# First experts and first head by halves of tokens, and weights requested at other moments, in a hybrid attention and expert stack

## The chip, the cores and the metric

The kernel runs on one core of one Trainium2 chip. Its time is the device time of one execution in microseconds; three executions were timed and the median is the measure. A profile of one more execution was taken with the hardware profiler. The engines are called PE (TensorE), DVE (VectorE), ACT (ScalarE), POOL (GpSimd) and SP (SyncE, which here only issues DMAs).

## What is computed

There are 1024 tokens of 512 numbers. Four layers follow each other, each on the layer norm of its input, added to that input:

```python
x = x + attention_a(layernorm(x), wq, bq, wk, bk, wv, bv, wo, bo)   # 32 heads of 16, 8 groups of keys
x = x + ffn(layernorm(x), W_base, b_base, W_router, A, B)
x = x + attention_b(layernorm(x), scales_q, ..., qw_q, qw_k, qw_v, qw_o)
x = x + ffn(layernorm(x), W_base, b_base, W_router, A, B)           # same weights again
```

Attention B has 32 heads of 128 in 8 groups of keys and values, is causal, and holds its weights as whole numbers 0 to 15, to be shifted by 8 and scaled per 128 input rows:

```python
w = (qw.astype(float32) - 8) * repeat(scales, 128, axis=0)
q, k, v = x @ w_q, x @ w_k, x @ w_v            # then rotary embedding of q and k:
q = q * cos + concat(-q[64:], q[:64]) * sin    # (per head; k likewise)
attn = softmax(where(causal, q @ k.T / sqrt(128), min))
out = (attn @ v) @ w_o
```

The feed-forward layer is one dense product and a low-rank part of rank 16 with 8 experts of which each token takes the best two:

```python
base = xf @ W_base.T + b_base
rw, sel = top_k(xf @ W_router.T, 2);  rw = softmax(rw)
lora = einsum('ter,te,eor->to', einsum('td,erd->ter', xf, A), onehot_weights(rw, sel), B) * 2
```

## The kernel before

The kernel has four stages on one core: attention A up to about 480 us, the first experts from 484 to about 535, attention B with its 32 heads to about 1418, and the second experts to the end.

**Who sets the order.** In attention B and both experts the order of PE's instructions is the order of the source. DVE, ACT, POOL and SP are ordered by the scheduler of the tile framework, which puts an instruction where its inputs and buffers are due; each engine then works through its own queue in order. A DMA that SP issues must wait, with everything behind it in SP's queue, until its source is written and its target buffer is free.

**First experts** (class `Experts`, L577 to L670). For each of eight tiles of 128 tokens, `hidden` computes the low-rank rows and the router's logits (L595), `route` picks the two experts on DVE for a range of tiles, `turned` transposes the weighted rows (evacuated by L134), `base` is the dense product (L607) and `finish` adds the low-rank product (L668) and adds the sum to x (L670). Each quarter of x (two tiles) that is complete is written to `x_kept` in DRAM, normalized (`ready`, L149 to L162), and turned into `x_hl`, a high and a low part of x transposed (`halves_of_x`, L185 and L754 to L756). Before, routing was done for tiles 0 to 5 and then for 6 and 7.

**Attention B's projections.** `whole_numbers` loads raw weights r from DRAM (L705, on SP) and POOL makes w = r - 8 from them (L706). Buffers: two of r and two of w for queries and for keys with values, one of r and two of w for the output weights. `scaled` multiplies w with x_hl, high and low part in turn (L798, L799), one PSUM bank for each 128 input rows, and gathers the four with their scales (L810 on ACT for the first, L812 on DVE for the others). `rotated` does it for 512 tokens at a time, then exchanges the halves of the head by two DMAs (`turned`, L822 and L823), and computes acc * cos + turned * sin in three operations (L824 to L826): on POOL, except for the queries of head 0, which are rotated on DVE.

**A head.** `probabilities(n, t)` computes the scores of query tile t of 128 tokens (L869), the mask and the row maximum in one DVE operation (L877), and the exponential on ACT (L881). `divided` is a reciprocal of the row sums (L885) and a scaling on ACT (L886). `placed` transposes 32 x 32 blocks on DVE (L900), and behind an odd tile of a pair four DMAs move the blocks to their rows (L911). `context` multiplies them with the values (L949), and `project_out` with the output weights (L798, L799), gathered on DVE into yT (L983). The scores have one wide PSUM buffer and one narrow one; five PSUM banks serve all else.

**The written order.** For each head, eight turns: `TURNS` gives the order of tiles, 0, 6, 1, 7, 2, 4, 3, 5, and head 0 had its own, 0, 1, 2, 4, 3, 5, 6, 7. Between scores, `fill` takes shares of other work from two lists, `short` (projections) and `long` (context and turned values); `advance` takes one step of one of their items and `complete` the whole. The tiles of `x_sb` are reused for the probabilities, in the slots named by `SLOTS` and `LAST`.

**Requests of weights.** At the start of head n, the source requested the query and output weights of head n+1, and at certain heads the keys' or values' weights of the next group (L1076 to L1083). The experts' weights lay in `shared` until attention B took that space; they are kept in DRAM (`w_kept`) and come back into the space of `x_hl` by one load after the last head's turns (L1137, L1138).

## Time and profile before

| what | us |
|---|---|
| three runs | 1474.58, 1474.74, 1477.38 |
| median | 1474.74 |
| profiled execution | 1478.29 |
| span of its instructions | 1476.5 |
| PE busy | 1398.8 (95%) |
| DVE busy | 1228.7 (83%) |
| ACT busy | 832.4 (56%) |
| POOL busy | 460.6 (31%) |

The span is the time from the first to the last instruction of the profiled execution, and the execution's own time has 1.8 us around it. A line such as `pc L949` means an instruction of line 949 of the kernel which writes the tile `pc`. In a timeline, the first two numbers are the start and the duration, and brackets hold the time that the engine sat idle before it and what ended that wait. `SPq` stands for SP's queue. Busy times are averages over stages; the stages are read from windows. The granted clock (PEclk) is the share of full speed that PE was given in a window.

### The profile page before, as it was taken

To read this page: it belongs to the slowest core of one execution; us is meant where nothing else is said; L and a number is where in the kernel's file an instruction comes from. 1 tells how busy PE (TensorE), PEld (TensorE's weight loads), DVE (VectorE), ACT (ScalarE), POOL (GpSimd) and SP (SyncE) were. 2 spreads that over 40 slices of the span, in tenths; PEclk is the share of its full clock that TensorE was granted. 3 is DMA by queue.
4 is the path that set the end of the run, shared out by engine and by line. 5 is a ranking of instruction groups with operands and counts; after the bars stand their busy time and mean duration, and the time that the engine had idled before them with its cause. 6 is when DMAs were issued, how large, how long until landed. Compare 5 with 4: busy or idle time off the path is not lost.

```text
span 1476.5 us, 21101 instructions
## 1 busy us (share of the span) xinstructions
PE 1398.8 (95%) x6711; PEld 884.2 (60%) x6711; DVE 1228.7 (83%) x2546; ACT 832.4 (56%) x1580; POOL 460.6 (31%) x363
## 2 busy tenths in 40 slices
PE   6999999999999998999999999999999999999788
PEld 4444444444444555677776776776776766777564
DVE  4799979889891668799998998998998989989683
ACT  2176757666676335765655655655665655666420
POOL 3200000000000516536445355445445535433120
PEclk9999999999999999999999999999999999999999
DMA  4352414223330415555555555545655555555511
GB/s 124 59 104 46 68 34 70 45 50 60 53 118 2 126 57 143 138 135 147 146 136 134 138 133 140 146 119 143 154 126 130 137 144 128 131 134 155 137 45 57
DMA packets 135870, 158.46 MB, mean 107 GB/s; under 512 B 34912, under 2 KB 111392, under 8 KB 135504
## 3 DMA queue, kind: packets, MB, share of 16 engines
q1 hardware_dynamic: 135340, 156.49, 44.6%
q8 instruction: 54, 0.88, 0.2%
q0 software_dynamic: 352, 0.59, 0.1%
q14 instruction: 56, 0.46, 0.1%
q10 hardware_dynamic: 68, 0.03, 0.0%
HBM read 33.03 MB, written 6.05 MB: 26 GB/s over the span
## 4 chain that ended last, share of the span: by engine, by line
PE 63%; DVE 15%; DMA 9%; ACT 4%; issue 3%; POOL 3%; SPq 3%; DVEq 0%; ACTq 0%; POOLq 0%
PE pc L949 11%; PE sc L869 10%; PE po L408 7%; PE sc L334 7%; DVE m L343 6%; DMA xT<-blocks 5%; PE pp L798 4%; PE pp L799 3%; PE bank L607 3%; DMA turned<-acc 3%; PE py L798 2%; PE py L799 2%; SPq L911 2%; PE st L375 2%; PE py L448 2%
## 5 line engine op out<-in xcount | busy, mean ns | idle before, releaser
L343 DVE TENSOR_REDUCE m<-sc 128x1 f32<-128x512 f32 x512 | 319.8, 682 | 25.8 <-PE st L375 20.1
L387 ACT ACTIVATE pT<-st 128x512 f32<-128x512 f32 x512 | 264.7, 602 | 128.6 <-PE st L383 115.6
L869 PE MATMUL sc<-kT,qT 128*128 128x512 f32 (+3 forms) x768 | 291.4, 488 | 4.1 <-DVE qT L826 1.7
L949 PE MATMUL pc<-xT,v_sb 128*128 128x256 f32 (+1 forms) x1024 | 243.4, 364 | 28.5 <-DMA xT<-blocks 26.0
L881 ACT ACTIVATE x_sb<-x_sb,m 128x768 f32<-128x768 f32 (+7 forms) x256 | 196.9, 769 | 124.8 <-DVE m L877 121.0
L886 ACT ACTIVATE x_sb<-x_sb,total 128x768 f32<-128x768 f32 (+7 forms) x256 | 194.2, 770 | 120.1 <-DVE total L885 120.0
L949 PEld LDWEIGHTS pc<-xT,v_sb 128*128 128x128 f32 x1024 | 192.0, 191 | 65.7 <-issue 28.7
L877 DVE CUSTOM_DVE_ANT_0 x_sb<-sc,causal 128x768 f32<-128x768 f32 (+7 forms) x256 | 191.2, 747 | 34.1 <-PE sc L869 33.5
L334 PE MATMUL sc<-ks,qs 64*128 64x512 f32 x512 | 186.8, 448 | 5.3 <-DVE m L343 2.5
L798 PE MATMUL pp<-x_hl,w 128*128 128x512 f32 x384 | 185.6, 483 | 5.9 <-ACT acc L810 5.2
L869 PEld LDWEIGHTS sc<-kT,qT 128*128 128x128 f32 x768 | 138.9, 192 | 75.6 <-issue 61.2
L383 PE MATMUL st<-ms_q,ones 64*128 64x512 f32 x512 | 178.0, 413 | 0.7 <-DMA ms_q<-mT 0.7
L375 PE MATMUL st<-qs,ks 64*128 64x512 f32 x512 | 175.9, 423 | 1.4
L983 DVE SCALAR_TENSOR_TENSOR shared<-py,o_sc,shared 128x512 f32<-128x512 f32 x248 | 173.8, 731 | 2.0 <-PE py L799 2.0
L334 PEld LDWEIGHTS sc<-ks,qs 64*128 64x128 f32 x512 | 83.8, 184 | 146.1 <-DVE m L343 129.5
L824 POOL TENSOR_TENSOR qT<-acc,cos_sb 128x512 f32<-128x512 f32 x62 | 79.8, 1287 | 248.6 <-DVE acc L812 246.4
L799 PE MATMUL pp<-x_hl,w 128*128 128x512 f32 x384 | 154.0, 401 | 2.4 <-DVE x_hl L756 2.4
L900 DVE STREAM_TRANSPOSE blocks<-x_sb 128x640 f32<-128x640 f32 (+3 forms) x128 | 133.3, 1041 | 21.4 <-ACT x_sb L886 14.7
L706 POOL TENSOR_SCALAR w<-r 128x512 fp32r<-128x512 int32 x80 | 119.4, 1492 | 93.8 <-PE pp L799 49.7
L812 DVE SCALAR_TENSOR_TENSOR acc<-pp,q_sc,acc 128x512 f32<-128x512 f32 x192 | 140.3, 731 | 9.6 <-ACT acc L810 8.7
L798 PE MATMUL py<-ctx,w 128*128 128x512 f32 x256 | 133.6, 522 | 3.4 <-DVE shared L983 1.1
L408 PE MATMUL po<-pT,v_sb 128*32 128x512 f32 x1024 | 136.6, 604 | 0.0
(171 smaller groups left out, 1889.2 us busy)
## 6 DMA issues: line engine op xcount, KB each, us to landing
xT<-blocks SPq DMA_DIRECT2D x128, 240.0 KB, 4.4
xT<-blocks SPq DMA_DIRECT2D x128, 176.0 KB, 3.4
turned<-acc SPq DMA_DIRECT2D x160, 128.0 KB, 2.7
pT<-x_sb SPq DMA_DIRECT2D x128, 112.0 KB, 2.5
qs<-q_hl SPq DMA_DIRECT2D x128, 64.0 KB, 2.4
qs<-shared SPq DMA_DIRECT2D x128, 64.0 KB, 2.5
r<-in_qwq_dram SPq DMA_DIRECT2D x32, 256.0 KB, 2.8
r<-in_qwo_dram SPq DMA_DIRECT2D x32, 256.0 KB, 2.8
```

The lines of the kernel that those rows point to most:

```text
L334: nc.tensor.matmul(sc, qs[pair % NS][rows, jj, ts(t, P)], ks[pair // 2 % NS][rows, ts(half, C)], start=True, stop=True,)
L343: nc.vector.tensor_reduce(ms[pair][:, at : at + 1], sc, AX.X, ALU.max, negate=True)
L375: nc.tensor.matmul(st, ks[pair // 2 % NS][rows, ts(kt, P)], qs[pair % NS][rows, u // 2, ts(u % 2, C)], start=True, stop=False,)
L387: nc.scalar.activation(pTs[pair, kt][:, u], st, AF.Exp, scale=DA**-0.5)
L408: nc.tensor.matmul(po[ts(u, 32), :], v_sb[:, kt, pair // 2, :], pT[:, u], start=(kt == 0), stop=(kt == NT - 1),)
L798: nc.tensor.matmul(ps, lhsT, high, start=True, stop=False)
L799: nc.tensor.matmul(ps, lhsT, low, start=False, stop=True)
L869: nc.tensor.matmul(sc[:, k0:k1], qT[:, ts(t, P)], kT[:, k0:k1], start=True, stop=True)
L877: nc.vector.tensor_tensor_reduce(p, sc[:, :keys], causal[:, S - keys :], -1.0, BIG, ALU.add, ALU.min, m)
L881: nc.scalar.activation(p, p, AF.Exp, bias=m, scale=-1.0, accum_out=total)
L886: nc.scalar.activation(p, p, AF.Copy, scale=total)
L949: nc.tensor.matmul(pc[:, 2 * P * i + lo : 2 * P * (i + 1)], v_sb[:, k, ts(g, DB)], some, start=(k == 0), stop=(k == 2 * pair + 1),)
```

## The change

1. Weights: the queries' raw weights of heads 0 and 1 are requested at the start; those of head n+1 at the start of head n as before, from head 1 on; the output weights of head n at its third turn; the keys' and values' weights at the fifth turn of the head before the one in which they were requested (`request`).
2. First experts: routing is done by halves, tiles 0 to 3 and 4 to 7; the two tiles of a quarter are computed and finished together; the normalized rows lie in a part of `v_sb` in place of tiles of their own.
3. First head: the first halves (512 tokens) of the keys, of queries 0 and of queries 1 are issued within the experts (`half_of`), and the first four query tiles of head 0, which need only the first half, stand ahead of the last quarter of x and of the second halves. The second half of the keys of group 0 is rotated on DVE and not on POOL. Head 0 takes its tiles in order 0 to 7, with the wide scores buffer for the odd ones; `SLOTS` is 0, 1, 3.
4. The experts' weights come back in seven pieces of at most 128 x 517 numbers, one in each of the last head's turns but the first (`reload`); each is behind a one-column copy on DVE which ties it to that turn's row sums.

```diff
@@ weights at the start
-            wqs = {0: input_weights("q", qwq, 0)}
+            wqs = {n: input_weights("q", qwq, n) for n in range(2)}
@@ keys
-                yield from rotated(kTs[g], wks.pop(g), lambda c: k_sc[:, c, g : g + 1])
+                engines = nc.gpsimd, nc.gpsimd if g else nc.vector
+                yield from rotated(kTs[g], wks.pop(g), lambda c: k_sc[:, c, g : g + 1], engines)
@@ probabilities
-                wide = t >= NT // 2 or (n == 0 and t == 1)
+                wide = t >= NT // 2 or (n == 0 and t % 2 == 1)
-            SLOTS = 0, 3, 1
+            SLOTS = 0, 1, 3
@@ first experts
-                    xns = [sb.tile([P, 2, C], F32, name=f"xn{i}") for i in range(2)]
+                    xns = [v_sb[:, 2 * i : 2 * i + 2, C:] for i in range(2)]
+                    def half_of(lane, name):
+                        item = [q for q in lane if q[0] == name][0]
+                        for _ in range(5):
+                            advance(lane, item)
-                    moe.route(0, 6)
-                    moe.route(6, 8)
...
+                    moe.route(0, 4)
...
+                    moe.finish(3)
+                    ready(1)
+                    moe.route(4, 8)
...
-                    for item in list(short):
-                        while advance(short, item):
-                            pass
+                    half_of(short, ("k", 0))
+                    half_of(short, ("q", 0))
                     moe.finish(6)
                     moe.finish(7)
                     ready(3)
                     halves_of_x(2, xns[0])
-                    short.append([("v", 0), 16 * FAST, values(0)])
-                    for _ in range(4):
-                        advance(short, short[-1])
-                    halves_of_x(3, xns[1])
+                    half_of(short, ("q", 1))
@@ before the heads
+                def reload(i, total):
+                    flat = x_hl.rearrange("p i c s -> p (i c s)")
+                    room = place_ffn_weights(flat.bitcast(F32))
+                    width = -(-room.shape[1] // (NT - 1))
+                    part = slice(i * width, min((i + 1) * width, room.shape[1]))
+                    nc.vector.tensor_copy(flat[:, part.start : part.start + 1], total)
+                    nc.sync.dma_start(room[:, part], w_kept[:, part])
+                def request(n):
+                    g, j = n // J, n % J
+                    if j == 0 and 0 < g < G - 1:
+                        wks[g + 1] = input_weights("k", qwk, g + 1)
+                    if j == 2 and g + 1 < G:
+                        wvs[g + 1] = input_weights("k", qwv, g + 1)
+                divided(*turn(0, 0))
+                divided(*turn(0, 1))
+                half_of(short, ("v", 0))
+                halves_of_x(3, xns[1])
+                divided(*turn(0, 2))
+                complete(("k", 0))
+                complete(("q", 0))
+                divided(*turn(0, 3))
+                complete(("v", 0))
+                complete(("q", 1))
+                wks[1] = input_weights("k", qwk, 1)
@@ a head
-                        wqs[n + 1] = input_weights("q", qwq, n + 1)
-                        wos[n + 1] = whole_numbers("o", qwo[ts(n + 1, P), :], C)
+                    if 0 < n < HEADS - 1:
+                        wqs[n + 1] = input_weights("q", qwq, n + 1)
+                        if n and i == 2:
+                            wos[n] = whole_numbers("o", qwo[ts(n, P), :], C)
+                        if i == 4:
+                            request(n + 1)
                         fill(short, shares[0])
                         divided(p, total)
+                        if n == HEADS - 1 and i:
+                            reload(i - 1, total)
@@ after the heads
-                weights = place_ffn_weights(x_hl.rearrange("p i c s -> p (i c s)").bitcast(F32))
-                nc.sync.dma_start(weights, w_kept)
```

`turn(n, t)` issues the scores and exponential of one tile, and places the tile before it, as the loop did.

## The prediction

> **What bounds the kernel now.** I read the page first: the busy shares, then the chain of work that ended last.
>
> ```profile
> span 1476.5 us, 21101 instructions
> ...
> PE 1398.8 (95%) x6711; PEld 884.2 (60%) x6711; DVE 1228.7 (83%) x2546; ACT 832.4 (56%) x1580; POOL 460.6 (31%) x363
> ...
> PE 63%; DVE 15%; DMA 9%; ACT 4%; issue 3%; POOL 3%; SPq 3%; DVEq 0%; ACTq 0%; POOLq 0%
> ```
>
> TensorE is busy 95% of the span, so at most 1476.5 - 1398.8 = 77.7 us is idle time, and an edit that does not change the matmuls can only win from it. The average hides where it lies, so I asked next for windows around the two places that the diff touches. Columns: from:to, length, busy us of PE, PEld, DVE, ACT, POOL, then granted TensorE clock, DMA share, GB/s.
>
> ```profile
> 540.00:560.00 20.00, 15.77 (x55) 10.45 (x53) 17.23 (x37) 10.24 (x20) 9.16 (x7) 0.83 0.29 92
> 560.00:580.00 20.00, 15.78 (x60) 9.88 (x59) 18.79 (x38) 14.05 (x23) 13.78 (x11) 1.00 0.51 128
> ...
> 1360.00:1380.00 20.00, 13.24 (x47) 10.11 (x46) 11.78 (x27) 6.48 (x12) 4.06 (x4) 0.83 0.71 210
> ```
>
> There are two weak places. From 540 to 580 (last of the first experts, first head of attention B) PE loses 8.4 of 40 us while VectorE is at 17.2 and 18.8 of 20: VectorE is the bound there. From 1360 to 1380 (head 30 to head 31) PE loses 6.8 us and VectorE idles too, while the DMA engines are at 0.71: a transfer bounds it. The timeline of PE names the waits, in square brackets behind an instruction:
>
> ```profile
> 543.19 0.80 PE L799 MATMUL pp<-x_hl,w 128*128 128x512 f32 x1 [2.38 <-DVE x_hl L756]
> 562.10 1.35 PE L869 MATMUL sc<-kT,qT 128*128 128x512 f32 x4 [1.73 <-DVE qT L826]
> 1370.93 1.62 PE L949 MATMUL pc<-xT,v_sb 128*128 128x256 f32 x3 [6.76 <-DMA xT<-blocks]
> ```
>
> A long wait costs twice. In the windows after the first and the third of these the granted clock is 0.50 for 3.41 us or twice that:
>
> ```profile
> 543.04:546.45 3.41, 2.56 (x6) 1.59 (x6) 3.41 (x10) 0.86 (x2) 0.00 (x0) 0.50 0.12 49
> 1369.08:1372.50 3.42, 1.57 (x4) 1.33 (x5) 0.00 (x0) 0.00 (x0) 0.88 (x1) 0.50 0.74 192
> ```
>
> Last, the waits in the steady heads (620 to 1385), on PE and in SyncE's queue (total, times, longest):
>
> ```profile
> PE pc L949 <- DMA xT<-blocks: 20.7, 12, 6.8
> ```
> ```profile
> SPq L705 <- POOL w L706: 140.0, 67, 11.3
> ```
>
> So in 30 heads PE waits 20.7 us for turned blocks of probabilities, and SyncE stands 140 us behind raw-weight loads that wait for a buffer which GpSimd has not yet converted.
>
> **The change part by part.** The sum is made on the profiled execution, 1478.29 us (span 1476.5 and 1.8 around it), which lies 3.55 above the median of 1474.74; differences are carried over to the median.
>
> *Raw weights at other moments (L1076, L1077, L1080, L1083).* Comparing the built programs engine by engine, from the end of the first head to the start of the last one PE's instructions stand in the same order, GpSimd's too but for one swap, and SyncE's differ in six heads, where one transfer xT<-xT goes ahead of r<-in_qwo. In those heads the transfers of blocks behind it wait for the transpose L900 anyway: for instance it ends at 726.63 and they are issued at 726.68. The reason is that a load is placed when its buffer is free, not when the source asks. So the two waits above stay: 0 us, with 1.5 either way for clock windows that fall otherwise.
>
> *First experts by halves (L1013 to L1053).* The same matmuls. Two waits for the turned hidden rows (L668 on L134) of some 0.75 each, by the way ACT's copy follows the transposes, stand where 0.24 and 0.68 are now; VectorE's longer route over four tiles ends near 497.1, while PE is on base (L607) until 499.3, so that is covered, and without this cover it would be up to 1 us. +0.2 (0 to +0.4). Behind the third quarter of x, queries of head 1 stand where the values stand now, and wait for the same L756: the 2.38 us stay.
>
> *Head 0's first four tiles ahead, k0 rotation on VectorE (L815, L824 to L826).* The work up to the transpose of 1024 columns (L900, 580.04 to 581.29) bounds this stretch, since the blocks that PE waits for leave after it. From 545.64 to 581.29 VectorE is busy 31.62 of 35.65 us. Three operations come over from GpSimd. Their row on VectorE is 0.69, 0.69 and 0.68: +2.06, so 33.68. Of the 4.03 idle now, waits for ACT of 0.77, 0.59 and 0.58 are partly filled by the new work, and a new wait arises: L825 needs the turned half by DMA, 0.5 to 1.1 us by what VectorE and GpSimd wait at 560.09 and 557.17. I take 3.0 idle: 545.64 + 33.68 + 3.0 = 582.3, which is +1.0, and PE, waiting for the blocks at 589.40, takes it in full. Ends: -1.5 if the first four tiles cut the idle time to half a microsecond beyond the new work, +4 if that wait and the queue behind it grow.
>
> One rule of the Trainium skill speaks against this move ("SBUF — State Buffer", SBUF: two separate sides): a VectorE operation with two SBUF inputs and a GpSimd operation that reads SBUF lock each other out of a shared port for a whole instruction. The trace has the pair:
>
> ```profile
> 540.26 1.02 DVE L824 TENSOR_TENSOR qT<-acc,cos_sb 128x512 f32<-128x512 f32 x1
> ```
> ```profile
> 539.44 1.29 POOL L825 TENSOR_TENSOR turned<-turned,sin_sb 128x512 f32<-128x512 f32 x1 [1.72 <-DMA turned<-acc]
> 540.81 1.60 POOL L826 TENSOR_TENSOR kT<-kT,turned 128x512 f32<-128x512 f32 x1
> ```
>
> VectorE's product took 1.02 beside GpSimd's L825, against 0.69 alone, and GpSimd's next 1.60 against 1.29. By the rule at its worst, three waits of 1.29, this part would be +3.9 more; by the row it is 0.3 each when they meet, and they need not meet three times. I go by the row, within the 3.0.
>
> PE is nearly without work from some 559 to 565 in the new order (scores of tile 4 wait for the values' and queries' first terms, L810 and L812), so one more half-clock window is likely: 1.7 us at full loss (half of 3.41), at one chance in five beyond those of now, +0.3.
>
> Here a second rule matters ("TensorE: Matmul & The Clock Gate", Part 1): the clock falls after an idle window of about 3.4 us, with the advice to allow no gap over about 3. By it the waits of 2.38 us would be free of a clock loss. The row at 543.04 shows 0.50 behind a wait of 2.38 us. I therefore price every wait above 2 us with a clock loss, as likely as the wait fills most of one window; by the rule the sum below would be 0.7 lower (0.3 here, 0.4 at the end).
>
> *The experts' weights in seven pieces (L1137, L1138).* Now one load of 128 x 3616 floats, 1.85 MB, stands before the blocks of the last head but one:
>
> ```profile
> 1357.56 0.53 SPq L1138 DMA_DIRECT2D x_hl<-w_kept  x1
> 1360.06 1.21 SPq L911 DMA_DIRECT2D xT<-blocks  x2
> 1365.12 0.34 SPq L705 DMA_DIRECT2D r<-in_qwo_dram  x1
> 1365.52 1.19 SPq L911 DMA_DIRECT2D xT<-blocks  x2
> 1366.75 1.17 SPq L822 DMA_DIRECT2D turned<-acc  x1
> ```
>
> Two of four blocks issues go at 1360.06; then SyncE stands 3.9 us behind an L705 held by GpSimd's conversion (1363.61 to 1365.10), which itself waits for PE. In the new program that load is behind all four blocks and the turned halves come first. Blocks are issued from 1360.06 (the transpose ends at 1360.04) to 1363.9, and land 3.3 us after, as at the next such place: PE resumes at 1367.2 in place of 1370.93: -3.7. The wait left, some 3.0 us, can still cost a clock window: two windows at 0.50 now cost about 2.5 us (PE work of 1.57 + 3.40 at half speed), one at 0.7 chance costs 1.2: -1.3. Against it: the transpose of 1024 columns of head 31 stands behind the mask of 640 columns (0.79) and copies: +0.9, with PE's wait before 1396.74 growing from 2.05 to 3 and thus +0.4 of clock. Seven copies of one column (0.15 each by the reciprocal of the same form, 0.07 from start to start) with three ahead of blocks: +0.2. Seven DMAs of 265 KB beside the blocks in place of one: +0.3. The first use of these weights is past 1400, so they are in time both ways. Sum -3.2, between -6 and -0.5.
>
> Total: 0.2 + 1.0 + 0.3 + 0 - 3.2 = -1.7, and 1474.74 - 1.7 = **1473.0**.
>
> **The rivals.** *Faster, 1470.* The first head comes out even: head 0's four tiles fill VectorE's waits for ACT, so 2.06 us of new work fit into 4.03 idle. At the end 3.0 us of wait cost no clock window: -3.7 - 2.5 + 0.9 + 0.2 + 0.3 = -4.8, so 1469.9. For it: every wait there has a name that the new order takes away. Against: VectorE at 18.8 of 20.
>
> *Slower, 1479.* One mechanism: the turned half of k0 is late on VectorE. Today its wait stops only GpSimd; after the change L825 sits in VectorE's queue, with the masks L877, the sums L812 and so PE behind it. Its transfer (L822) is in SyncE's queue, where L705 waits up to 11.3 us for GpSimd. Each microsecond beyond the wait assumed is one at the transpose, plus up to 1.7 for a clock window. It decides from 4.7 us beyond the sum (1473.0 to 1477.7); at 6 it ends at 1479.0. A stand of SyncE of half its longest, 5.6 us, would do it. Against it: before, such waits around 557 to 560 were 1.1 at most.
>
> *It doesn't do what it says, 1476.* The raw weights do not move, as shown, and the seven pieces carry the same 1.85 MB beside the same blocks (DMA at 0.71), so that the wait at 1364 stays over 5 us: -3.2 becomes 0, and 0.2 + 1.0 + 0.3 remain: 1476.2.
>
> **How the numbers follow.** A change under 0.2% (2.95 us) can hardly be told from none here, so the bounds are 1471.8 and 1477.7. Chances: the sum as reckoned 0.42 (its own range 1470.5 to 1476, thus 0.12 faster, 0.28 same, 0.02 slower), the faster rival 0.25, the slower 0.24, the idle one 0.09. Faster 0.37, same 0.37, slower 0.26. The range goes to 1467.5 (ends of the bounds -1.5 and -6 near together) and to 1480 (the slower rival with one clock window more).
>
> **What would show it.** Right: PE's wait before L949 near 1367 about 3 us, blocks issued in one run from about 1360; the transpose of 1024 columns of head 0 ending 0 to 2 us later than now against the first L826; the waits of L705 on L706 still near 140 us. Wrong: VectorE waiting over 4 us for the turned halves between 545 and 582; more windows at 0.50 before 620; steady heads shifting by more than 2 us in sum; a wait for the experts' weights after 1400.

## The result and the profile after

The change made the kernel slightly slower. Over 19 executions of each on the same chips the median is 1481.13 us after and 1477.13 before, a ratio of 1.0024 [1.0013, 1.0034], some 3.5 us. The forecast had said 1.7 us faster. The profiled execution took 1479.78 us, with this on its page:

```profile
span 1478.0 us, 21133 instructions
...
PE 1398.0 (95%) x6711; PEld 883.4 (60%) x6711; DVE 1231.3 (83%) x2556; ACT 833.0 (56%) x1580; POOL 457.3 (31%) x360
...
PE 64%; DVE 14%; DMA 9%; ACT 4%; issue 3%; SPq 3%; POOL 3%; DVEq 0%; ACTq 0%; POOLq 0%
```

The shares tell nothing here; in the chain by engine none moved by more than one point. The windows of after at the same clock times as those shown of before (from:to, length, busy us of PE, PEld, DVE, ACT, POOL, then granted clock, DMA share, GB/s) show one place won and one lost:

```profile
540.00:560.00 20.00, 15.03 (x55) 10.34 (x55) 18.13 (x42) 9.84 (x20) 9.31 (x7) 0.91 0.30 86
560.00:580.00 20.00, 16.22 (x48) 9.33 (x48) 17.37 (x33) 11.91 (x18) 9.35 (x7) 0.83 0.50 124
...
1360.00:1380.00 20.00, 16.94 (x73) 12.65 (x72) 17.16 (x41) 11.70 (x24) 7.86 (x6) 1.00 0.59 138
```

At the end of the heads PE's busy time rose from 13.24 to 16.94 us and the clock from 0.83 to 1.00. From 560 to 580 PE looks busier than before (16.22 against 15.78), yet it executed 48 matmuls in place of 60: the clock fell from 1.00 to 0.83, so part of that busy time is the same work taking longer.

To place the difference I cut the two traces at instructions that both have, so that a shift of attention A (the experts start at 485.93 before and at 484.30 after) drops out. "Clock" is half of PE's busy time in windows granted 0.50, that is, what full speed would have saved by this reckoning. Context products (L949 before, L950 after, two per head) are counted by VectorE's gathering of their sums. The stretch from the 5th to the 8th, 38.44 and 38.48 us, is left out.

| from, to | before: length, PE idle, clock | after | change | forecast |
|---|---|---|---|---|
| experts' start, first projection | 45.97, 1.03, 0 | 45.99, 1.46, 0 | 0.0 | +0.2 |
| to the 5th context product ("first heads") | 109.24, 13.07, 3.00 | 113.30, 14.41, 6.12 | +4.1 | +1.3 |
| 8th to 10th (beside head 4) | 27.68, 0.29, 0 | 29.84, 2.24, 0 | +2.1 | 0 |
| 10th to 58th ("steady heads") | 634.92, 22.35, 5.05 | 635.03, 23.80, 3.41 | +0.1 | 0 |
| 58th to 64th ("end of heads") | 71.02, 10.97, 2.49 | 67.66, 8.68, 1.71 | -3.4 | -3.2 |
| to the end | 63.31, 9.13, 1.71 | 63.39, 9.19, 1.71 | +0.1 | 0 |

So what was expected at the end came, and two losses ahead of it took it back. PE's timeline of after names the waits:

```profile
541.79 0.50 PE L799 MATMUL pp<-x_hl,w 128*128 128x512 f32 x1 [2.59 <-DVE x_hl L756]
562.55 0.80 PE L798 MATMUL pp<-x_hl,w 128*128 128x512 f32 x1 [3.54 <-ACT acc L810]
591.13 5.17 PE L950 MATMUL pc<-xT,v_sb 128*128 128x256 f32 x16 [2.32 <-DMA xT<-blocks]
685.90 1.10 PE L950 MATMUL pc<-xT,v_sb 128*128 128x256 f32 x4 [1.96 <-DMA xT<-blocks]
1371.74 1.10 PE L950 MATMUL pc<-xT,v_sb 128*128 128x256 f32 x4 [3.06 <-DMA xT<-blocks]
1396.61 1.10 PE L950 MATMUL pc<-xT,v_sb 128*128 128x256 f32 x4 [3.48 <-DMA xT<-blocks]
```

In the first heads there are now three waits above 2 us where there was one, and the one of 3.54 is new. Behind it and behind the one at 591 the clock is at half (windows of after):

```profile
561.40:564.80 3.40, 2.25 (x4) 1.00 (x4) 3.04 (x5) 1.38 (x2) 0.00 (x0) 0.50 0.40 108
564.80:568.20 3.40, 3.24 (x8) 2.01 (x8) 3.35 (x6) 0.68 (x1) 1.49 (x1) 0.50 0.48 119
...
592.10:595.50 3.40, 3.40 (x10) 2.69 (x9) 1.42 (x4) 2.38 (x4) 2.38 (x2) 0.51 0.08 17
```

What is late ahead of 562.55 is the turned half of k0. SyncE's queue, GpSimd, VectorE and ScalarE of after, one fence each:

```profile
555.88 0.54 SPq L705 DMA_DIRECT2D r<-in_qwk_dram  x1
557.25 0.39 SPq L705 DMA_DIRECT2D r<-in_qwq_dram  x1
557.72 0.53 SPq L822 DMA_DIRECT2D turned<-acc  x1
```
```profile
555.73 1.49 POOL L706 TENSOR_SCALAR w<-r 128x512 fp32r<-128x512 int32 x1 [0.52 <-PE pp L799]
```
```profile
555.56 0.74 DVE L812 SCALAR_TENSOR_TENSOR acc<-pp,k_sc,acc 128x512 f32<-128x512 f32 x1
...
561.76 0.69 DVE L825 TENSOR_TENSOR turned<-turned,sin_sb 128x512 f32<-128x512 f32 x1 [1.66 <-DMA turned<-acc]
```
```profile
561.81 0.69 ACT L810 ACTIVATE acc<-pp,v_sc 128x512 f32<-128x512 f32 x1 [0.95 <-DMA turned<-acc]
```

The sum to be exchanged is ready at 556.30 (555.56 + 0.74). SyncE stands until 557.22 at a load of raw weights whose buffer GpSimd is still converting, so the exchange leaves at 557.72, 1.4 us late, and lands about 4 us later. VectorE waits 1.66 us for it, and so does ScalarE: the values' first sum goes into the buffer of `acc` which that DMA still reads. PE waits for ScalarE to free its bank. This is the mechanism of the forecast's slower rival, at a smaller size, so it is tested first.

### The profile page after: what moved, and what is told of

It reads as the page before. It is cut to its first block, busy times and chain, and to the rows that moved or that the text cites. A ratio compares the mean times of both kernels' runs of the same rounds, so it can differ in the third digit from the quotient of the medians.

```text
span 1478.0 us, 21133 instructions
## 1 busy us (share of the span) xinstructions
PE 1398.0 (95%) x6711; PEld 883.4 (60%) x6711; DVE 1231.3 (83%) x2556; ACT 833.0 (56%) x1580; POOL 457.3 (31%) x360
## 4 chain that ended last, share of the span: by engine, by line
PE 64%; DVE 14%; DMA 9%; ACT 4%; issue 3%; SPq 3%; POOL 3%; DVEq 0%; ACTq 0%; POOLq 0%
PE pc L950 12%; PE sc L870 11%; PE po L408 7%; PE sc L334 7%; DVE m L343 6%; DMA xT<-blocks 6%; PE pp L798 4%; PE pp L799 4%; PE bank L607 3%; SPq L912 3%; PE py L798 2%; PE py L799 2%; DMA turned<-acc 2%; PE st L375 2%; PE py L448 2%
## 5 line engine op out<-in xcount | busy, mean ns | idle before, releaser
L950 PE MATMUL pc<-xT,v_sb 128*128 128x256 f32 (+1 forms) x1024 | 243.4, 363 | 31.1 <-DMA xT<-blocks 28.5
L950 PEld LDWEIGHTS pc<-xT,v_sb 128*128 128x128 f32 x1024 | 191.8, 191 | 68.5 <-issue 33.5
L706 POOL TENSOR_SCALAR w<-r 128x512 fp32r<-128x512 int32 x80 | 119.7, 1496 | 93.9 <-PE pp L799 48.6
```

The source lines that it names most:

```text
L950: nc.tensor.matmul(pc[:, 2 * P * i + lo : 2 * P * (i + 1)], v_sb[:, k, ts(g, DB)], some, start=(k == 0), stop=(k == 2 * pair + 1),)
```

## Experiments

Every kernel was run beside the kernel before on the same chip. The ratio is to before, with its 95% interval. "First heads", "head 4" and "end" are the lengths of the table above in the profiled execution (before: 109.2, 27.7, 71.0). Each execution also reports its span and its mean clock. Within a kernel, over 399 executions, 0.001 less of mean clock goes with 1.05 us more of span (correlation -0.83). The last two columns use that slope to part the mean span's distance from before (179 executions, 1475.5 us at 0.9903) into clock and the rest; this parting is good to some 0.1 us, and it is a correlation, not a cause shown. The lengths contain whatever clock loss their one execution had: the end's 72.0 in k0_pool has 5.9 us of it, so the columns of lengths are read with the two last ones.

| kernel | ratio to before | first heads | head 4 | end | clock part | rest |
|---|---|---|---|---|---|---|
| after | 1.0024 [1.0013, 1.0034] | 113.3 | 29.8 | 67.7 | +1.5 | +2.0 |
| pieces_alone | 0.9988 [0.9976, 0.9999] | 107.8 | 27.9 | 70.4 | -0.5 | -1.2 |
| pieces_undone | 1.0026 [1.0015, 1.0037] | 113.3 | 29.6 | 68.8 | +1.2 | +2.6 |
| k0_pool | 1.0038 [1.0024, 1.0053] | 113.4 | 31.5 | 72.0 | +2.5 | +3.2 |
| v_acc_apart | 1.0031 [1.0017, 1.0045] | 113.0 | 30.3 | 70.7 | +0.9 | +3.7 |
| loads_held | 1.0031 [1.0019, 1.0043] | 118.0 | 27.8 | 67.7 | +3.1 | +1.5 |
| second_half_first | 1.0017 [1.0003, 1.0031] | 112.5 | 29.8 | 67.5 | -0.5 | +2.9 |
| conversion_late | one execution | 109.6 | 27.9 | 71.5 | | |
| pieces_early | 0.9978 [0.9966, 0.9990] | 108.9 | 27.7 | 68.0 | -1.5 | -2.1 |
| second_first_k0_pool | 1.0053 [1.0033, 1.0074] | 114.2 | 31.7 | 71.7 | +4.5 | +3.2 |
| second_first_q1_later | 1.0009 [0.9999, 1.0018] | 113.6 | 28.1 | 70.3 | +0.6 | -0.1 |
| k0_vector_alone | 1.0005 [0.9990, 1.0019] | 113.0 | 28.2 | 71.5 | +0.8 | -0.2 |
| pieces_moments | 0.9983 [0.9969, 0.9996] | 108.3 | 27.6 | 68.9 | -0.3 | -2.4 |
| halves_alone | 0.9993 [0.9981, 1.0006] | 110.3 | 28.4 | 70.8 | +0.2 | -0.2 |
| halves_undone | 1.0030 [1.0018, 1.0042] | 111.7 | 32.8 | 68.8 | +3.0 | +2.7 |
| after_warm | 0.9979 [0.9963, 0.9995] | 110.4 | 27.7 | 68.0 | -3.4 | +1.1 |
| kept_warm | 0.9976 [0.9962, 0.9989] | 109.1 | 27.8 | 67.3 | -8.3 | +5.9 |
| kept_warm2 | 0.9941 [0.9923, 0.9958] | 108.3 | 27.9 | 65.2 | -8.7 | +0.1 |

### The end: the seven pieces

**pieces_alone** puts the seven pieces into the kernel before, and nothing else.

```diff
+                        if n == HEADS - 1 and i:
+                            reload(i - 1, total)
...
-                weights = place_ffn_weights(x_hl.rearrange("p i c s -> p (i c s)").bitcast(F32))
-                nc.sync.dma_start(weights, w_kept)
```

> The kernel before with one part of the change: the experts' weights come back in seven pieces during the last head. Theory (the end of the change is worth what the trace of after shows there, -6.3 us at the first wait of L949 and +3.2 at the second): 3 us faster than before, ratio 0.998, first wait at the end about 3.0 in place of 6.8 us, second 3.5 in place of 2.1; head 2 has no wait of 2 us before L949. Rival (the gain needs the output weights requested later): the first wait stays over 6 us and the time is within 1 us of before.

Ratio 0.9988, by which 1.8 us are won; PE's waits at the end are 3.47 and 3.75 us in place of 6.76 and 2.05. The first wait fell nearly to the 3.0 reckoned, the second rose.

**pieces_undone** is after, with the one load in place of the pieces.

```diff
-                        if n == HEADS - 1 and i:
-                            reload(i - 1, total)
...
+                weights = place_ffn_weights(x_hl.rearrange("p i c s -> p (i c s)").bitcast(F32))
+                nc.sync.dma_start(weights, w_kept)
```

> The changed kernel with the experts' weights in one load of 1.85 MB again. In its order of DMAs this load stands ahead of four blocks' transfers in one run, and r<-in_qwo is behind the turned halves. If what made the first wait long was SyncE standing at r<-in_qwo between the blocks' transfers, the wait at the end stays near 3 us and the time is that of after (1.002 to 1.003 of before). If it was the 1.85 MB on the DMA engines, the wait is 5 to 7 us and the time 2 to 3 us over after (1.004 to 1.005 of before).

Ratio 1.0026, hardly more than after's 1.0024, since in this order the load costs less: PE's timeline shows the first wait grown from 3.06 to 5.10 only, as the blocks' four transfers now leave in one run and share the DMA engines with the load, and the second fell from 3.48 to 2.13.

```profile
1373.20 2.05 PE L950 MATMUL pc<-xT,v_sb 128*128 128x256 f32 x4 [5.10 <-DMA xT<-blocks]
```

Neither expectation was met whole. By time the pieces win 1.8 us in the old order (pieces_alone) and 0.3 us, which is none within the intervals of 1.6 us, in the new one (after beside pieces_undone). Removing them does not remove the loss.

**pieces_early** asks whether the second wait (3.75) comes from pieces that travel beside the blocks. It is pieces_alone with two pieces in each of three turns and one in a fourth, meant to leave earlier.

```diff
-                        if n == HEADS - 1 and i:
-                            reload(i - 1, total)
+                        if n == HEADS - 1 and 0 < i < 5:
+                            for k in range(2 * i - 2, min(2 * i, NT - 1)):
+                                reload(k, total)
```

> The kernel before with the experts' weights in seven pieces, two in each of the last head's second to fourth turns and one in the fifth, so that none leaves beside the last transfers of 480-wide blocks. If the pieces beside the blocks make the second wait at the end long (3.5 to 3.8 us with pieces in each turn, 2.05 with one load before), it falls to 2 to 2.5 us and the time is 1 to 2 us under that of the pieces in each turn. If what delays the blocks is the transpose behind the mask of 640 columns, the wait stays over 3 us and the time is the same as with pieces in each turn (0.999 of before).

It has the lowest ratio of the versions without added work, 0.9978, though not clear of pieces_alone, and the second wait stays. PE's timeline, SyncE's queue and VectorE of this kernel:

```profile
1391.60 1.64 PE L949 MATMUL pc<-xT,v_sb 128*128 128x256 f32 x4 [3.56 <-DMA xT<-blocks]
```
```profile
1382.81 1.01 SPq L1079 DMA_DIRECT2D x_hl<-w_kept  x2
1383.98 3.95 SPq L911 DMA_DIRECT2D xT<-blocks  x4
```
```profile
1381.95 0.80 DVE L877 CUSTOM_DVE_ANT_0 x_sb<-sc,causal 128x640 f32<-128x640 f32 x1
1382.68 1.24 DVE L900 STREAM_TRANSPOSE blocks<-x_sb 128x1024 f32<-128x1024 f32 x1
```

The edit did not do what it was meant to do: two pieces leave just ahead of these blocks, so the traffic was not taken away. Its size can be read all the same. From the blocks' first issue to PE's resumption pass 7.62 us here (1383.98 to 1391.60), 7.52 in pieces_alone, and 7.12 in before (1389.62 to 1396.74), where no piece travels: some 0.5 of the 1.5 us by which the wait grew. The rest arises ahead of the issue. There the wide transpose stands behind the mask of 640 columns (0.80), as the forecast had it (+0.9), and in before and in pieces_undone, with waits of 2.05 and 2.13, it stands ahead of that mask. The order was not changed alone.

**pieces_moments** adds the raw weights' moments of the change to pieces_alone.

```diff
+                        if n and i == 2:
+                            wos[n] = whole_numbers("o", qwo[ts(n, P), :], C)
+                        if i == 4:
+                            request(n + 1)
```

> The kernel before with the experts' weights in pieces and all raw weights requested at the moments of the change; experts and first head as before. If the moments are worth nothing, as the prediction had it, the steady heads and the end go as with the pieces alone: no wait of 2 us in head 4, first wait at the end 3 to 3.5, ratio 0.998 to 0.999. If they matter, for better or worse, the ratio is off that by 0.002 and the waits of L949 in the steady heads differ by more than 2 us in sum.

0.9983 beside 0.9988: with these experts and this first head, the moments bring and cost nothing that can be told from the noise.

### The first heads: is it k0 on VectorE?

**k0_pool** is after with the second half of k0 rotated on GpSimd, as before.

```diff
-                engines = nc.gpsimd, nc.gpsimd if g else nc.vector
+                engines = nc.gpsimd, nc.gpsimd
```

> The changed kernel with the second half of the keys of group 0 rotated on GpSimd again, all else kept. Theory (VectorE's queue bounds head 0: 2.06 us of rotation and a wait of 1.66 us for the turned half before L825): the transpose of 1024 columns ends 2.5 to 3.5 us earlier after the first L826, PE's wait of 3.5 us at some 562 shrinks, and the time is 1.5 to 3 us below after (about 1.0005 of before). Rival (the two buffers of acc hold the projections back until the turned halves have landed, whoever rotates): the 3.5 us wait of PE for L810 stays and the time is within 1 us of after.

It did not get better (1.0038 beside 1.0024), the transpose of 1024 columns ended 100.2 us after the experts' start (98.7 in after) and not 2.5 to 3.5 earlier, and the wait stayed, by PE's timeline of this kernel:

```profile
563.13 0.79 PE L798 MATMUL pp<-x_hl,w 128*128 128x512 f32 x1 [3.43 <-ACT acc L810]
```

The theory that VectorE's queue behind L825 carries the loss finds no support. By time, the move alone gives the same answer: **k0_vector_alone** is the kernel before with k0 on VectorE.

```diff
-                yield from rotated(kTs[g], wks.pop(g), lambda c: k_sc[:, c, g : g + 1])
+                yield from rotated(kTs[g], wks.pop(g), lambda c: k_sc[:, c, g : g + 1], (nc.gpsimd, nc.gpsimd if g else nc.vector))
```

> The kernel before with only this part of the change: the second half of the keys of group 0 is rotated on VectorE. VectorE is busy 31.5 of 35.6 us up to the transpose of 1024 columns. If its queue is the bound there, as the prediction had it, the transpose ends 1 to 2.1 us later (96.4 to 97.5 after the experts' start against 95.4 to 96.0) and the kernel is 1 to 2 us slower. If VectorE takes it up in its idle time, because the keys are there sooner than GpSimd delivers them (1.29 us an operation against 0.69), the transpose ends within 0.5 us of before or earlier, ratio 0.999 to 1.0005.

1.0005 [0.9990, 1.0019]: no change that can be measured. Its profiled execution alone would have said the opposite: 113.0 us in the first heads, with 5.85 of clock against 3.00 before, and the transpose of 1024 columns 98.9 us after the experts' start, as late as in after. Ten timed executions do not bear that out (+0.8 of clock, -0.2 of rest). One profile of the first heads can mislead by 3 us.

**v_acc_apart** takes the shared buffer away: the values' sums of group 0 go to a free part of `v_sb`, so ScalarE need not wait for the exchange of halves.

```diff
-                    acc = work.tile([P, C], F32, tag="acc", name="acc")
+                    acc = v_sb[:, 6 + half, C:] if g == 0 else work.tile([P, C], F32, tag="acc", name="acc")
```

> The changed kernel with the sums of the values of group 0 in an unused part of v_sb, so that only keys and queries share the two buffers of acc. If the buffers of acc are what makes PE wait 3.5 us for L810 at 562, that wait falls below 1.5 us, and the time falls by 1 to 2.5 us against after. If VectorE's queue is the bound, the wait may go but the transpose of 1024 columns of head 0 ends within 0.7 us of where it does in after, and the time is within 1 us of after.

The wait of 3.54 did shrink, and another one arose behind it, by PE's timeline:

```profile
561.41 0.50 PE L798 MATMUL pp<-x_hl,w 128*128 128x512 f32 x1 [1.57 <-DVE v_sb L812]
...
566.59 2.50 PE L870 MATMUL sc<-kT,qT 128*128 128x512 f32 x4 [2.75 <-DVE qT L826]
```

No gain (1.0031): PE now waits for the second half of the queries, which are as late as before. The buffer was a cause of that one wait; taking it away did not take away the loss.

**loads_held** holds the two loads that stood ahead of L822 until the row sums of head 0's fourth tile exist.

```diff
+                if after is not None:
+                    nc.vector.tensor_copy(r[:, 0:1].bitcast(F32), after)
...
+                wks[1] = input_weights("k", qwk, 1, total)
...
-                wks[1] = input_weights("k", qwk, 1)
```

> The changed kernel with two raw-weight loads held back: that of the keys of group 1 until the sums of query tile 3 of head 0, that of the queries of head 2 until those of tile 7 (a one-column copy on VectorE into the load's target ties them). With them gone from SyncE's queue ahead of the turned halves, and GpSimd's conversion ahead of the rotation no longer swapped in head 4. Theory (SyncE standing at these loads and their 512 KB beside the turned halves make the halves late): L825's wait of 1.66 us goes, the transpose of 1024 columns ends 2 to 3 us earlier after the experts' start (98.7 us in after, 95.4 in before), PE's wait of 3.5 us for L810 falls under 2, and the wait of 2 us before L950 at 686 goes: together 4 to 5 us below after, 0.999 of before. Rival (the halves are late because the second half of the tokens is projected later, whatever loads stand there): the transpose ends within 0.7 us of after, only the 2 us at 686 are won: 1.001 of before.

VectorE no longer waits for the turned half, so the loads were what made it late, and PE's wait for L810 shrank from 3.54 to 1.29 us. But the held weights then came late, and PE waited for them (PE's timeline):

```profile
586.92 0.80 PE L800 MATMUL pp<-x_hl,w 128*128 128x512 f32 x1 [7.87 <-POOL w L708]
```

The transpose of 1024 columns ended as late as in after (98.9 us after the experts' start). The loads cannot be held so long; what a shorter hold would give is open. Head 4 is at 27.8 us here, which a later part takes up.

**second_half_first** puts the last quarter of x and the second halves of k0 and q0 ahead of the first four tiles' remaining work.

```diff
-                divided(*turn(0, 0))
-                divided(*turn(0, 1))
-                half_of(short, ("v", 0))
                 halves_of_x(3, xns[1])
-                divided(*turn(0, 2))
+                p, total = turn(0, 0)
                 complete(("k", 0))
                 complete(("q", 0))
+                divided(p, total)
+                divided(*turn(0, 1))
+                half_of(short, ("v", 0))
+                divided(*turn(0, 2))
```

> The changed kernel with the last quarter of x and the second halves of keys and queries of head 0 again ahead of its tiles 1 to 3 (tile 0 stands ahead of the keys' second half as before); all else kept, and the two loads where they are. If putting four tiles ahead of the second half is what delays the scores of tile 4 (81.7 us after the experts' start against 76.2 in before), they come at 77 to 79 and the transpose of 1024 columns ends 2 to 3 us earlier than in after: 1.0005 to 1.001 of before. If the loads ahead of the turned halves are the cause, the scores of tile 4 still come after 80 and the time is that of after.

1.0017: by 12 executions the clock part is gone (-0.5) while the rest grew to +2.9. The transpose came 0.8 us earlier (97.9) and not 2 to 3. The interval overlaps that of after, so no gain is shown. **second_first_k0_pool** adds GpSimd's rotation to it.

```diff
-                engines = nc.gpsimd, nc.gpsimd if g else nc.vector
+                engines = nc.gpsimd, nc.gpsimd
```

> The changed kernel with two parts undone at once: the last quarter of x and the second halves of keys and queries of head 0 stand ahead of tiles 1 to 3 again, and the second half of the keys of group 0 is rotated on GpSimd. With the first alone the transpose of 1024 columns ended 97.9 us after the experts' start (98.7 in after, 95.4 to 96.0 in the four kernels with the old order of head 0). If what is left is the 2.06 us of rotation on VectorE, it ends at 95.5 to 96.2, and the stretch from the first projection to the last context of head 1 (109 us in the old order, 112.5 with the first part alone) falls to 109 to 110.5. If what is left is that the queries of head 1 and the values are finished before tile 4, so that PE has nothing to put into the waits of tiles 4 to 7, the transpose may come earlier but the stretch stays over 111.5. Head 4's wait of 2 us stays in both.

1.0053 by four executions, the slowest of all, with much of it in clock (+4.5) and 31.7 us at head 4. GpSimd's rotation did not help in this order either; why it is slower is not shown. **second_first_q1_later** leaves, besides that, the second half of queries 1 to head 0's fill (without `complete(("q", 1))`).

```diff
-                complete(("q", 1))
                 wks[1] = input_weights("k", qwk, 1)
```

> As the kernel with the second half first and the keys on GpSimd, and moreover the second half of the queries of head 1 is not finished ahead of tile 4 but left to fill the waits of tiles 4 to 7, as in the kernel before. GpSimd's conversion in head 4 also stands before the rotation again. If the lost filler is the cause, the stretch from the first projection to the last context of head 1 falls to 108.5 to 110 and the kernel is as fast as before less what the weights in pieces win at the end (0.9985 of before). If not, the stretch stays within 0.7 us of that with the queries finished early.

1.0009, but not for the reason hoped: the first heads are still 113.6 us, and head 4 fell to 28.1.

### Halves of the experts, or the first head?

**halves_alone** puts only the experts by halves into the kernel before; **halves_undone** is after with the experts of before. The first of them, cut:

```diff
-                    for t in range(6):
+                    for t in range(4):
                         moe.hidden(t)
...
-                    moe.route(0, 6)
-                    moe.route(6, 8)
+                    moe.route(0, 4)
...
+                    moe.finish(3)
                     ready(1)
+                    moe.route(4, 8)
```

> The kernel before with the first experts by halves alone (routing of tiles 0 to 3 and 4 to 7, two tiles of a quarter together, rows in v_sb), head 0 and all else as before. If the experts by halves are free, as the prediction had it (0 to 0.4 us), the stretch from the first projection to the last context of head 1 is 107.8 to 109.7 us and the ratio 0.9995 to 1.0005. If they bring the loss by shifting what VectorE does at the last quarter of x, the stretch is over 112 us and the ratio 1.002 to 1.003.

The second, cut:

```diff
-                    moe.route(0, 4)
...
+                    moe.route(0, 6)
+                    moe.route(6, 8)
...
-                    moe.route(4, 8)
```

> The changed kernel with the first experts in the order of before, and head 0 by halves as in the change. If the loss comes with head 0, the stretch stays at 112.5 to 114 us and the ratio at 1.002 to 1.003. If it comes with the experts by halves, the stretch falls to 108 to 110 us and the ratio to 1.000 (head 4's wait of 2 us and the end's gain stay).

0.9993 and 1.0030. By time the halves of the experts are free, and without them the loss is all there: it comes with head 0's new order and with what that order does later. In the trace of halves_undone the first heads lose to clock alone (6.20 of 111.73, and 105.5 without it, where before has 106.2), and head 4 is the longest of all, 32.8.

### Head 4: a swap that had been priced at nothing

The forecast had seen one swap in GpSimd's order and costed it at 0. GpSimd before, then after, at head 4:

```profile
671.61 1.49 POOL L706 TENSOR_SCALAR w<-r 128x512 fp32r<-128x512 int32 x1 [0.71 <-PE py L799]
...
674.37 1.29 POOL L825 TENSOR_TENSOR turned<-turned,sin_sb 128x512 f32<-128x512 f32 x1 [1.27 <-DMA turned<-acc]
```
```profile
673.38 1.30 POOL L825 TENSOR_TENSOR turned<-turned,sin_sb 128x512 f32<-128x512 f32 x1
674.75 1.27 POOL L826 TENSOR_TENSOR qT<-qT,turned 128x512 f32<-128x512 f32 x1
676.11 1.49 POOL L706 TENSOR_SCALAR w<-r 128x512 fp32r<-128x512 int32 x1
```

The conversion of output weights went behind the second rotation of queries 5, and ends at 677.60. The load that needs its buffer stands in SyncE's queue ahead of the blocks that PE waits for (before, then after):

```profile
673.12 0.35 SPq L705 DMA_DIRECT2D r<-in_qwo_dram  x1
673.58 3.55 SPq L911 DMA_DIRECT2D xT<-blocks  x4
```
```profile
677.63 0.35 SPq L705 DMA_DIRECT2D r<-in_qwo_dram  x1
678.09 3.90 SPq L912 DMA_DIRECT2D xT<-blocks  x4
```

The two traces are 2.45 us apart here, so the blocks left 2.06 us late (678.09 - 673.58 - 2.45) though their transpose was done at 675.99; PE's wait of 1.96 at 685.90 and the 2.1 us of the table answer to it.

**conversion_late** makes the same conversion late in the kernel before, but issues the load behind the blocks.

```diff
+                    if n == 4:
+                        w, r = behind_q[0]
+                        nc.gpsimd.tensor_copy(w[:, 0:1], qTs[5][:, C : C + 1])
+                        nc.gpsimd.tensor_scalar_add(w, r, -ZERO)
+                        wos[5] = whole_numbers("o", qwo[ts(5, P), :], C)
```

> The kernel before with one conversion of output weights (L706, head 4's, near 672) put behind the second rotation of queries 5 on GpSimd, as it stands in after, while SyncE has the blocks' transfers ahead of the load that waits for that conversion (in after they are behind it). If the 2.1 us that after loses at 686 come from SyncE standing at this load in front of the blocks, nothing is lost here: no wait over 0.5 us before the line of pc between 670 and 695. If the late conversion itself costs, some 2 us are lost there as in after.

Head 4 is 27.9 us, no loss, in its one execution. So GpSimd's late conversion is harmless by itself; the load that waits for it ahead of the blocks in SyncE's queue makes the price. The traces of the variants agree: after and the six others with the swap have 29.6 to 32.8 us at head 4, and the three without it (loads_held, second_first_q1_later, after_warm) 27.7 to 28.1. No kernel is after with the swap alone undone.

### The clock

Across the traces, the kernels with the old head 0 but k0_vector_alone and halves_alone (before, conversion_late, the three with pieces) have on average 108.8 us in the first heads, of which 3.2 is clock; the eight with the new one, without loads_held and after_warm, 113.1, of which 5.7. By these, 2.6 of the 4.3 us lost there are clock, and 1.8 are not. (With the two that were left out, at 113.0 and 110.3, it is 2.2 of 3.5.) **after_warm** tests that by giving PE work in the waits: unread matmuls of 512 columns, 9 and 13 of them, ahead of the waits of 2.59 and 3.54 us, and 14 of 256 columns ahead of that of 2.32. Nothing is left out.

```diff
+            def busy(bank, left, right, times):
+                for _ in range(times):
+                    nc.tensor.matmul(bank, left, right, start=True, stop=True)
...
+                busy(sc_ps.tile([P, C], F32, tag="scFalse", name="sc"), x_hl[:, 0, 0, 0:P], x_hl[:, 0, 1, 0:C], 13)
                 complete(("q", 1))
```

> The changed kernel with matmuls whose results nobody reads in three of PE's waits: 9 and 13 of 512 columns ahead of the waits of 2.6 us (for x_hl) and 3.5 us (for L810), 14 of 256 columns ahead of that of 2.3 us (for the blocks at 591), each about 1.7 to 3 us at full clock. In its order the conversion in head 4 also stands ahead of the rotation again. If half clocks after these waits are what makes the stretch longer, their cost in the stretch falls from 6.1 us to under 2, and the stretch from 113.3 to 109.5 to 111 us. If the waits only move, the cost falls but the time without PE's use grows by as much and the stretch stays over 112.5.

0.9979 [0.9963, 0.9995]: where after loses, this kernel gains, median 1474.16 beside 1477.93. The window that holds the first heads, of after, then of after_warm:

```profile
544.00:600.00 56.00, 47.41 (x167) 32.26 (x168) 43.48 (x90) 31.29 (x55) 24.70 (x19) 0.88 0.40 98
```
```profile
544.00:600.00 56.00, 49.77 (x205) 34.30 (x205) 46.07 (x95) 33.47 (x59) 26.72 (x20) 1.00 0.45 109
```

The clock is 1.00 in place of 0.88, and VectorE gets through 95 instructions and not 90 in the same time. In the first heads 6.1 us of clock are gone, PE's idle time fell by 4.7, and the unread matmuls took 7.4 on PE's timeline (2.34, 3.13 and 1.91): -6.1 - 4.7 + 7.4 = -3.4, of which the stretch shows -2.9 (113.3 to 110.4). At head 4 another 2.1 went (29.8 to 27.7), as the swap is gone by the way. These are 5.0 us in the two profiles; by the ratios the two kernels are 6.6 us apart, and the timed runs cannot part that between clock and swap. Nor does 110.4 beside the old order's 108.8 measure the order: the one has unread matmuls and no clock loss, the other has 3.2 of clock loss.

**kept_warm** takes the faster of the old-order kernels, pieces_early, and puts 8 unread matmuls of 256 columns into the waits for blocks in heads 8, 12 and so on to 28, 30 and 31, and 8 of 512 at 543.

```diff
+                    if which == 0 and i == 1 and n in (8, 12, 16, 20, 24, 28, 30, 31):
+                        busy(pc[:, 2 * P :], v_sb[:, 0, ts(g, DB)], v_sb[:, 0, 0 : 2 * P], 8)
...
+                    busy(sc_ps.tile([P, C], F32, tag="scFalse", name="sc"), x_hl[:, 0, 0, 0:P], x_hl[:, 0, 1, 0:C], 8)
```

> The kernel before with the experts' weights in early pieces and eight matmuls whose results nobody reads ahead of each wait of 2 us or more for blocks (heads 8, 12, 16, 20, 24, 28, 30, 31) and ahead of that for x_hl at 541. If such waits cost a half clock by chance, as the granted clock shows (0 to 5 us in the steady heads, by run), this cost falls to about 0 and the kernel is 3 to 5 us faster than with the early pieces alone: 0.995 to 0.996 of before. If the waits move (the extra 1.6 us run when the blocks are there already), it is no faster: 0.998.

In the steady heads and the end no window is at half any more, and still nothing is won beyond pieces_early (0.9976, 0.9978): the steady heads took 637.7 us in place of 635.4, as eight of these matmuls took 3.62 us on PE's timeline where the waits were about 2.1. Clock part -8.3, rest +5.9.

**kept_warm2** fits them to the waits: 4 in the steady heads, 7 at the end, and 8, 4 and 5 of 512 columns in head 0.

```diff
-                        busy(pc[:, 2 * P :], v_sb[:, 0, ts(g, DB)], v_sb[:, 0, 0 : 2 * P], 8)
+                        busy(pc[:, 2 * P :], v_sb[:, 0, ts(g, DB)], v_sb[:, 0, 0 : 2 * P], 4 if n < 30 else 7)
...
+                        if n == 0 and t == 4:
+                            busy(sc_ps.tile([P, C], F32, tag="scFalse", name="sc"), x_hl[:, 0, 0, 0:P], x_hl[:, 0, 1, 0:C], 5)
```

> As the kernel with early pieces and matmuls without a use in PE's waits, but with four of them (1.7 us) in each steady wait of some 2.1 us in place of eight (3.45 us), seven (3.0 us) in the two at the end of 3.1 and 3.6, and 4 and 5 of 512 columns ahead of head 0's waits for x_hl's last quarter and for the queries. If the half clocks were the cost, the steady heads show none and take 629 to 631 us (634.9 in before, 637.7 with eight), the end 66 to 67 (71.0): together 0.995 to 0.9965 of before. If a partly covered wait still drops the clock, one or more windows of 0.5 remain in the steady heads and the ratio is that of the early pieces, 0.998.

0.9941 [0.9923, 0.9958], median 1469.2 beside 1477.56: 8.4 us faster than before on the same chip, of which the early pieces alone make some 3.3 (0.9978). Its waits on PE for blocks in the heads (620 to 1385; total, times, longest) are this, where after has 20.8 us, since the unread matmuls now fill most of them:

```profile
PE pc L955 <- DMA xT<-blocks: 8.2, 12, 1.3
```

The window over the heads, first of before and then of kept_warm2:

```profile
640.00:1360.00 720.00, 696.96 (x2878) 514.37 (x2876) 661.93 (x1386) 434.01 (x815) 347.93 (x264) 0.99 0.56 136
```
```profile
640.00:1360.00 720.00, 705.15 (x2940) 521.77 (x2939) 665.41 (x1394) 436.37 (x819) 351.08 (x266) 1.00 0.56 136
```

## Why the prediction was wrong

Two steps failed, and in the profile they make up the distance between forecast and measurement. The swap on GpSimd, costed at nothing, measured +2.1 us. The clock loss beside head 0, put at +0.3, measured +3.1. The other terms came out within 0.2 of their sizes there, the end by some luck.

**Experts by halves, +0.2.** Right: 0.0 in the trace, and halves_alone is 0.9993 [0.9981, 1.0006].

**Raw weights' moments, 0.** Right for the moments (pieces_moments), wrong for the sentence on the swap. The step "GpSimd's too but for one swap", costed at 0, is the first that failed: +2.1 us. I had looked at whether the blocks wait for their transpose at the places where a load and a transfer change places on SyncE, and not at the place where the load stands ahead of the blocks in both orders but GpSimd frees its buffer later. A sign that the forecast named was missed as well: the waits of L705 on L706 were to stay near 140 us and fell to 121.9 (longest 4.3 in place of 11.3):

```profile
SPq L705 <- POOL w L706: 121.9, 65, 4.3
```

**Head 0, +1.0.** As a term it came out, but not by its path. Without clock, the first heads of the two profiles are 106.2 and 107.2 us, +0.9; over the groups of kernels above it is 1.8. The path was wrong: the transpose of 1024 columns ends 3.1 us later than before against the first L826 (3.4 against the experts' start), and not 0 to 2 later. VectorE's busy time up to it was put at 33.68 and measured 34.12. Its idle time was put at 3.0 and measured 4.66; the wait for the turned half, bounded at 0.5 to 1.1, was 1.66 of it. The half clock from 561.4 to 568.2 lies inside this stretch: in after_warm, with the same operations on VectorE and the clock at 1.00, the transpose ends 96.8 us after the experts' start in place of 98.7. So VectorE's queue was not the bound that the forecast took it for, as k0_vector_alone says by time.

**Clock beside head 0, +0.3.** The step that failed most: +3.1 in the profile, +2.6 over the groups of kernels. I had given one chance in five to one window. With three waits above 2 us in place of one the clock cost 6.12 and not 3.00 (four windows at half in place of two), and after_warm shows that this part is real: with the waits filled it is 0. The choice of the row over the clock page's rule was right, and still too mild; by the rule, which allowed gaps of some 3 us, the sum would have been 0.7 lower and further off. (Of the windows at half that the forecast showed, the one at 1369.08 begins inside the wait of 6.76 us and not after it.) The forecast also began from idle time alone: an edit that leaves the matmuls as they are "can only win from it". Half clock lies in PE's busy time, and the filled waits won from that.

**The end, -3.2.** Right as a sum in the profile of after, -3.4, and in part by luck. The first wait was 3.06 for 3.0 forecast, and the second grew to 3.48 for 3.0. But in the twelve traces with pieces and unfilled waits the end takes 69.3 us on average, 1.9 less than the 71.2 of the four with the old order and one load. Idle time fell by 2.6; the clock loss, which the forecast had falling by 0.9, rose by 0.9 (2.3 to 3.3), and after's own 1.71 is the least of the twelve, shared by four. The timed ratios, 0.3 to 1.8 us or 3.3 in the early form, agree with the smaller gain.

Sum of the profile: 0.0 + 4.1 + 2.1 + 0.1 - 3.4 + 0.1 = +3.0. The spans differ by 1.5, as attention A happened to be 1.6 shorter. Over all executions the loss is 3.5 us, so the match of single terms to this one profile is not to be taken closer than a few us.

**The rivals.** The slower one gave 1479, and the loss of some 3.5 us is near its +4.3, with its mark in the trace: L705 ahead of L822, and L825 waiting. Its mechanism is not what decides, though. The wait was 1.66 where the rival needed several us beyond the sum; taking k0 off VectorE does not make the kernel faster, and putting it there alone costs nothing that can be measured. The same mechanism, SyncE standing at a load, did decide at head 4, where no rival had looked. The faster rival fell with the first heads, and the idle one with the first wait at the end, which is 3.06 and not over 5. VectorE's busy time came out 0.4 us above my count, so the port's lock cost nothing near the 3.9 us of the rule at its worst.

**What stays open.** The first heads' loss beyond the clock, 1.8 us over the groups of kernels (107.4 without clock, against 105.6), is not settled: halves_alone shows it in its trace (107.5) though not in its times, and halves_undone has none in its trace (105.5). Four undoings of single steps (k0's engine, the shared buffer, the loads, the order of the second half) did not take it away, each shifting the wait to the next thing that was late. The change also fills head 0's later turns with a quarter of the remaining work each in place of a fifth, which no run takes apart. Which waits first is not settled, nor why the scheduler's order at head 4 follows head 0's.

## What to carry to other kernels

When an order is changed, compare not only the orders of each engine but, for every instruction that moved, which DMA waits for it and what stands behind that DMA in the issuing queue. Price each wait on TensorE of about 2 us as the wait plus a chance of half a clock window of work for every window that falls, one by one. Here 17 kernels with six unfilled waits of 1.5 to 3.0 us in the steady heads lost 3.3 us of clock on average, so the chance was about one in three. A wait that can't be removed can be filled with unread matmuls of the same length; too long a filling gives the gain back.

## What the runs showed of the hardware

In every trace the granted clock changes only at the edges of windows of 3.41 us which lie on one grid. In the 19 traces, some 5,200 windows from 500 to 1440 us, no window at full clock in which PE's matmuls left more than 1.98 us idle was followed by another at full clock, and the least idle time after which a full clock fell was 1.65 us. Once at half, the clock stayed there after windows with 0.60 us idle or more, and came back after those with 0.59 or less. The ends of matmuls are modelled in the traces, so these limits are approximate. So a wait of 2 us costs up to 1.7 us more for each window at half, or nothing, by where the grid cuts it: the 2.38 us of before brought two such windows and 3.00 us. The steady heads lost between 0 and 6.6 us of clock in kernels whose waits there are much the same. By the correlation of -0.83 the clock goes with about 70% of the variance between executions of one kernel, such as after's 1475.05 to 1484.96. The Trainium skill ("TensorE: Matmul & The Clock Gate", Part 1) puts the fall behind an idle window of about 3.4 us, and its section "Why this matters for your kernels", not Part 1, has the advice to allow no gap over about 3. Here 1.65 to 1.98 us of idle time within a window were enough, and the measurement decides.

A second surprise was the price of the filling. Eight float32 matmuls of 256 columns are sixteen records on PE's timeline of kept_warm, two for each, and 3.62 us in all; nine of 512 columns with operands rounded to the type fp32r in after_warm are nine records and 2.34 us. So one of the former took 0.45 us, more than the 0.26 of one of the latter with twice the columns:

```profile
1367.42 3.62 PE L938 MATMUL pc<-v_sb 128*128 128x256 f32 x16
```
```profile
538.84 2.34 PE L939 MATMUL sc<-x_hl 128*128 128x512 f32 x9 [0.29 <-ACT x_hl L755]
```
